# PSUM banks of a second attention: who shares which of four

## The chip, the cores and the metric

The kernel runs on one core of a Trainium2 chip. Its time is the device time in microseconds of one execution; several runs are made, and the median is compared. The core has five engines with queues of their own: PE (TensorE, matmuls, with its weight loads shown as PEld), DVE (VectorE), ACT (ScalarE), POOL (GpSimd) and SP, which issues the DMAs. PE writes its results to PSUM, which has eight banks of 128 x 512 float32; DVE and ACT read them from there. A bank can be given to a new result only when all readers of the old one are done.

## What is computed

The reference is a decoder of two layers on x of 4 x 1024 x 256. Layer 0 is a causal attention with 16 heads of 16 and linear biases, a cross-attention over 77 context rows with 16 heads, and a gated feed-forward with quantised weights. Layer 1 is a power attention with decay, a cross-attention with 8 heads, and a gated feed-forward with blockwise FP4 rounding. The part around the change is the power attention of layer 1:

```python
S = jnp.einsum('bhtd,bhsd->bhts', Q, K)
Tm = DEG * jnp.log(jnp.abs(S) + EPS) + jnp.log(jnp.float32(scale))
Z = Tm + log_G[..., :, None] - log_G[..., None, :]     # log_G: cumulated log of the gates; causal mask
P = jnp.exp(Z - Z_rowmax)
y = jnp.einsum('bhts,bhsd->bhtd', P, V) / jnp.sum(P, axis=-1)[..., None]
```

With DEG = 2 the exponential of Tm is a square, so that P is (|S| + eps) squared times a decay that depends on the two positions.

## The kernel before

The whole computation is one program. Python generators (`A0`, `XA`, `F0`, `A1`, `XF`, ...) emit instructions, and `weave` (L1168) mixes two generators by fixed proportions, so that the attention of one batch row stands beside the cross-attention and the feed-forward of the row before. `schedule` (L1202) has two phases. In phase 0 the attention of layer 0 is the main strand. In phase 1 (`K.phase = 1`) the main strand is `A1`, the power attention, and the side strands are the rest of layer 0 for the last row, the projections of the next row (`A1_front`, which calls `qkv`, L264) and `XF`, the cross-attention and feed-forward of layer 1. After the last attention the feed-forward of the last row runs in four lanes. The order in which the generators emit is only a priority: a scheduler orders each engine's queue when the program is built, by durations that it assumes, and may move any instruction whose operands and buffers allow it. On the chip each engine then works its queue off in that fixed order.

PSUM tiles come from `p(tag)` (L155). It looks up the banks of a tag in `BANKS[self.phase]` (L131 to L134) and takes them in turn; the counter belongs to the tuple of banks, so tags with the same tuple share one turn. Each bank holds one tile at a time. The second dictionary is that of phase 1:

- S: scores of A1 (`scores`, L877). A unit is one key tile of 128 against up to 256 queries for four heads. Its matmuls are at L901, two heads to a tile of 128 x 2 x 256, so a unit has two S tiles. Each is emptied into P (four buffers) with the absolute value: three in four by DVE at L907, one in four by ACT at L905. ACT squares the whole of P at L909, and POOL multiplies diagonal units with the decay at L912. `pv` (L915) multiplies P with V at L930 into O, at least two units later (`LAG1` = 2).
- D: `decay` (L866) makes the decays of a chunk's two diagonal units one chunk ahead: two tiles, each two matmuls at L873 and an exponential by ACT at L874 into y1. `local` (L861) makes the queries' factor for two chunks: a matmul at L863 and an exponential at L864 into `ub`, of which there is one. `a1_gates` (L778) uses D once per row (L791 to L800).
- O: the products, a single bank (7). `out` (L934) empties it with L937, L939 and L940 into `ot`, using `ub`.
- U: the sums in `ot` are transposed at L943 to bring queries back to partitions; DVE takes reciprocals of the norms at L946 and scales at L948 into yy, which POOL adds to X at L950.
- Q: projections of `qkv`: transpositions of the normed input (L235), emptied at L179 and L180, matmuls at L191 inside `mm3`, emptied by ACT at L290, L304 and L306 and DVE at L291. The output projection of the last row of layer 0 uses Q as well (L450).
- T and W: the side strands' tiles, in banks 4 to 6. TB and WB: the same for lanes at the very end, when S, D, U and Q are out of use.

A chunk is 256 queries of four heads: two diagonal units and 2c others for chunk c. There are 64 chunks, 320 units, 640 S tiles.

Of the kernel before, what the change touches and what calls it, by code (L numbers as in the profile page):

```python
# [22 lines left out]
B, T, C = 4, 1024, 256  # L23
NT = T // 128
H = 16
D = 16
# [64 lines left out]
class Kern:  # L91
# [13 lines left out]
    def __init__(self, ctx, tc, ins, out, consts, nb=B):  # L105
# [24 lines left out]

    BANKS = (  # L131
        {"S": (0, 1), "M": (2, 3), "M0": (0, 1, 2, 3), "Q": (2, 3), "U": (0,), "D": (0, 1), "O": (7,), "T": (4, 5, 6), "W": (4, 5, 6)},
        {"S": (0, 1), "Q": (2, 3), "U": (2, 3), "D": (2, 3), "O": (7,), "T": (4, 5, 6), "W": (4, 5, 6), "TB": (0, 1, 2, 3), "WB": (0, 1, 2, 3)},
    )  # L134

    XL = {"xX": "yTh", "R2": "yTl", "M0": "WAh", "M1": "WAl", "U0": "qp", "U1": "qp", "E": "V", "xph": "qr", "xpl": "qr"}
# [1192 lines left out]
```

## Time and profile before

| What | us |
|---|---|
| median of 3 runs | 2400.75 |
| lowest, highest | 2393.45, 2407.63 |
| the profiled execution | 2399.32 |
| its span, first to last instruction | 2397.5 |
| PE busy over the span | 2149.5 (90%) |
| DVE, ACT, POOL busy | 1698.9 (71%), 1637.4 (68%), 1195.4 (50%) |
| first score matmul of A1 (L901) starts | 1262.5 |
| last score matmul of A1 starts | 2245.3 |

An engine is busy when one of its instructions is being executed; PE's instructions overlap, so its busy time is not time at its peak. Idle time of an engine is put down to the instruction that released the waiting one. Weight loads run ahead of their matmuls, so that one stall of PE can show in a row of PEld, in one of PE, or in both. What counts for the change is the stretch between 1262 and about 2250 us, in which the second dictionary of banks is in force for S, D, U and Q.

The costliest groups of that attention are L909 on ACT (320 instructions, 344.6 us), L907 on DVE (480, 285.7 us), L901 on PE (1280, 219.0 us) and L930 on PE in two groups, of which the larger has 3584 instructions and 171.4 us.

### The profile page before, as it was taken

The numbers are of one execution on the slowest core, as the hardware profiler recorded it, in microseconds if no ns is written. First come the engines' busy times: TensorE is split into PE (matmuls) and PEld (weight loads), VectorE is DVE, ScalarE is ACT, GpSimd is POOL, SyncE is SP. The second block draws the span as 40 slices with busy tenths as digits, with TensorE's granted clock in tenths as the row PEclk, the third lists the DMA queues.
The fourth block names the chain that finished last, engine by engine and source line by source line (L and its number), as shares of the span: only waits on it lengthen the run. The fifth ranks groups of instructions, "written<-read, shape, count | busy, mean of one in ns | idle before, by whom it ended". The sixth has DMA issues, their size and how long they took to land.

```text
span 2397.5 us, 51455 instructions
## 1 busy us (share of the span) xinstructions
PE 2149.5 (90%) x19110; PEld 1522.7 (64%) x19110; DVE 1698.9 (71%) x3781; ACT 1637.4 (68%) x4173; POOL 1195.4 (50%) x1942
## 2 busy tenths in 40 slices
PE   6898999998999998999989988899988998898886
PEld 5564557755667754676546765567766776676676
DVE  4776457677766787775756677778767786777776
ACT  4474456676756675665768978887678777888542
POOL 7322212254231442412545457777767787876664
PEclk9898899999999999899989999999999999999897
DMA  8975321223841337312252224412331224442000
GB/s 257 286 193 168 101 72 44 73 64 105 265 105 44 86 95 196 87 44 58 87 174 52 67 70 147 128 39 74 92 104 38 56 88 121 92 98 71 10 10 18
DMA packets 182697, 238.45 MB, mean 99 GB/s; under 512 B 16198, under 2 KB 165846, under 8 KB 175958
## 3 DMA queue, kind: packets, MB, share of 16 engines
q1 hardware_dynamic: 182446, 235.15, 35.5%
q8 instruction: 151, 2.47, 0.4%
q14 instruction: 100, 0.82, 0.1%
HBM read 152.62 MB, written 82.21 MB: 98 GB/s over the span
## 4 chain that ended last, share of the span: by engine, by line
PE 64%; DVE 13%; ACT 8%; DMA 7%; POOL 5%; issue 2%; SPq 1%; DVEq 0%; ACTq 0%; POOLq 0%
PE T L191 11%; PE W L191 9%; PE O L413 7%; PE Q L191 6%; PE O L930 6%; PE S L401 5%; PE M L352 5%; PE S L901 4%; DVE P L907 2%; DVE s_mt L357 2%; PE T L726 2%; PE W L633 1%; ACT P L909 1%; DMA KS<-c_alk 1%; PE M L356 1%
## 5 line engine op out<-in xcount | busy, mean ns | idle before, releaser
L357 DVE TENSOR_REDUCE s_mt<-M 128x1 f32<-128x512 f32 (+3 forms) x608 | 386.1, 655 | 103.9 <-PE M L356 76.2
L404 ACT ACTIVATE P<-S 128x512 f32<-128x512 f32 (+1 forms) x640 | 340.2, 563 | 149.4 <-PE S L401 93.0
L909 ACT ACTIVATE P<-P,eps 128x1024 f32<-128x1024 f32 x320 | 344.6, 1084 | 55.1 <-DVE P L907 52.5
L907 DVE TENSOR_REDUCE P<-S 128x512 f32<-128x512 f32 (+1 forms) x480 | 285.7, 611 | 83.9 <-PE S L901 61.8
L352 PE MATMUL M<-KS,QS 108*128 108x512 bf16 (+3 forms) x768 | 225.6, 339 | 43.3 <-DVE s_mt L357 27.5
L901 PE MATMUL S<-QS,KS 96*128 96x256 bf16 (+1 forms) x1280 | 219.0, 269 | 42.0 <-DVE P L907 35.9
L191 PE MATMUL T<-R,xX 128*128 128x352 f32 (+1 forms) x1136 | 246.8, 332 | 4.9 <-ACT E L622 1.9
L401 PE MATMUL S<-QS,KS 110*128 110x256 bf16 (+1 forms) x1280 | 230.7, 268 | 15.6 <-ACT P L404 8.0
L625 POOL TENSOR_TENSOR E<-E,s_xsm 128x616 f32<-128x616 f32 x64 | 77.8, 1217 | 316.9 <-DVE s_xsm L623 188.3
L413 PE MATMUL O<-P,V 128*32 128x256 f32 (+1 forms) x2560 | 231.4, 374 | 0.1
L191 PEld LDWEIGHTS T<-R,xX 128*128 128x128 f32 x1136 | 183.0, 190 | 25.6 <-ACT E L622 6.5
L912 POOL TENSOR_TENSOR P<-P,y 128x512 f32<-128x512 f32 x128 | 166.5, 1309 | 48.3 <-ACT P L909 28.1
L191 PE MATMUL W<-R,xph 128*128 128x256 f32 (+1 forms) x952 | 184.9, 292 | 3.3 <-ACT xph L179 2.6
L622 ACT ACTIVATE E<-T,s_xmx 128x77 f32<-128x77 f32 x512 | 159.4, 334 | 25.7 <-DVE s_xmx L619 23.0
L930 PE MATMUL O<-P,VsJ 128*32 128x128 f32 x3584 | 171.4, 286 | 5.6 <-ACT P L909 5.3
L901 PEld LDWEIGHTS <-KS 96*128 96x128 bf16 x1280 | 103.9, 99 | 113.4 <-issue 90.6
L401 PEld LDWEIGHTS <-KS 110*128 110x128 bf16 x1280 | 106.4, 100 | 104.9 <-issue 57.2
L191 PEld LDWEIGHTS W<-R,xph 128*128 128x128 f32 (+1 forms) x952 | 149.9, 192 | 12.1 <-issue 3.6
L352 PEld LDWEIGHTS <-QS 108*128 108x128 bf16 x768 | 68.1, 99 | 116.0 <-issue 88.2
L191 PE MATMUL W<-R,xpl 128*128 128x256 f32 (+2 forms) x476 | 139.1, 292 | 1.4 <-DVE xpl L180 1.2
L179 ACT ACTIVATE xph<-W 128x512 fp32r<-128x512 f32 (+2 forms) x180 | 79.6, 459 | 86.6 <-PE W L636 39.6
L733 POOL TENSOR_TENSOR R<-wst 128x256 f32<-128x256 f32 x128 | 92.4, 732 | 83.0 <-DVE wst L732 71.2
(353 smaller groups left out, 5683.8 us busy)
## 6 DMA issues: line engine op xcount, KB each, us to landing
QS<-dr SPq DMA_DIRECT2D x144, 192.0 KB
KS<-dr SPq DMA_DIRECT2D x72, 384.0 KB
dr<-qp SPq DMA_DIRECT2D x32, 768.0 KB
MD<-R SPq DMA_DIRECT2D x24, 616.0 KB
UD<-R SPq DMA_DIRECT2D x24, 512.0 KB
R<-MD SPq DMA_DIRECT2D x32, 308.0 KB
X<-in_x SPq DMA_DIRECT2D x16, 512.0 KB
dr<-qp SPq DMA_DIRECT2D x32, 256.0 KB
```

Of the source, the lines that this page charges most:

```text
L191: nc.tensor.matmul(out, x, y, start=first and n == 0, stop=last and n == len(seq) - 1)
L352: nc.tensor.matmul(Sv[:, x, 0:w], QS[:108, i // 4, hh, i % 4 * 128 : i % 4 * 128 + 128], KS[:108, hh, k0:k1], start=x == 0, stop=not diag ...
L357: nc.vector.tensor_reduce(out, Sv[:, :, 0:w], AX.X, ALU.max)
L401: nc.tensor.matmul(S[:, e, 0:w], st[1][:110, hh, j * 128 : (j + 1) * 128], st[0][:110, q0 // 512, hh, q0 % 512 : q0 % 512 + w], start=e == ...
L404: nc.scalar.activation(P[:, 2 * p : 2 * p + 2, 256 - w :], S[:, :, 0:w], AF.Exp)
L413: nc.tensor.matmul(O[0][hh * 32 : hh * 32 + 32, o + o0 : o + 256], V[j // 4][:, j % 4, h * 17 : h * 17 + 32], P[:, hh, o0:], start=c % 2 = ...
L622: nc.scalar.activation(E[:, n * 77 : (n + 1) * 77], Sv[:, k, :], AF.Exp, bias=mx[:, n : n + 1], accum_out=sm[:, n : n + 1])
L901: nc.tensor.matmul(S[:, e, 0:w], st[r][1][:96, hh, j * 128 : (j + 1) * 128], st[r][0][:96, q0 // 512, hh, q0 % 512 : q0 % 512 + w], start= ...
L907: nc.vector.tensor_reduce(Pv, S[:, :, 0:w].unsqueeze(3), AX.X, ALU.max, apply_absolute_value=True)
L909: nc.scalar.activation(Pw, Pw, AF.Square, bias=self.eps1)
L912: nc.gpsimd.tensor_tensor(Pd, Pd, Ds[r, c][:, j - 2 * c], ALU.mult)
L930: nc.tensor.matmul(Oc[rows, o0 : o0 + 128], lhs, P[:, hh, c0 : c0 + 128], start=j == 2 * c and i == 2 * c, stop=fin and i == 2 * c + 1)
```

## The change

One line of the table of banks, that of phase 1, is replaced.

```diff
     BANKS = (
         {"S": (0, 1), "M": (2, 3), "M0": (0, 1, 2, 3), "Q": (2, 3), "U": (0,), "D": (0, 1), "O": (7,), "T": (4, 5, 6), "W": (4, 5, 6)},
-        {"S": (0, 1), "Q": (2, 3), "U": (2, 3), "D": (2, 3), "O": (7,), "T": (4, 5, 6), "W": (4, 5, 6), "TB": (0, 1, 2, 3), "WB": (0, 1, 2, 3)},
+        {"S": (0, 1, 2), "Q": (2, 3), "U": (3,), "D": (3,), "O": (7,), "T": (4, 5, 6), "W": (4, 5, 6), "TB": (0, 1, 2, 3), "WB": (0, 1, 2, 3)},
     )
```

Before, S turned over banks 0 and 1, and Q, U and D together over 2 and 3. After it, S turns over 0, 1 and 2; U and D turn over bank 3 alone; Q has its own turn over 2 and 3, so every second Q tile lies in a bank of the scores and the others in that of U and D. Nothing else in the source differs. Since the scheduler orders queues by what buffers allow, the order of instructions on every engine differs from the point where phase 1 begins.

## The prediction

> **What bounds the kernel now.** I read the table of stages first, then the waits inside the changed stage, then the costliest groups. The changed table is in force only in the second attention, whose first score matmul starts at 1262 us and whose last evacuation ends near 2248 us, so I cut the span there (columns: stretch, length, then busy us of PE, weight loads, DVE, ACT, POOL, then granted clock, DMA share, GB/s):
> ```profile
> 0.00:1262.00 1262.00, 1143.77 (x8997) 746.99 (x8997) 864.78 (x1910) 785.10 (x2180) 426.61 (x623) 0.96 0.44 124
> 1262.00:2246.00 984.00, 891.29 (x9409) 670.09 (x9405) 732.91 (x1673) 796.42 (x1832) 679.44 (x1216) 0.96 0.31 82
> 2246.00:2397.50 151.50, 114.43 (x708) 105.62 (x708) 101.22 (x200) 55.91 (x162) 89.36 (x104) 0.85 0.03 11
> ```
> In the middle stage PE is busy 891 of 984 us, ACT 796, DVE 733. PE is the bound, closely followed by ACT. PE executes in order, so all that a PSUM bank can give or take here lies in PE's idle 93 us. The waits of that stage say what the idle time waits for (engine, what waited, what it waited for: total us, times, longest us):
> ```profile
> DVE P L907 <- PE S L901: 61.8, 83, 2.2
> PE S L901 <- DVE P L907: 35.9, 55, 3.8
> PEld O L930 <- POOL P L912: 10.0, 23, 1.3
> PEld O L930 <- ACT P L909: 8.3, 24, 1.2
> PE O L930 <- ACT P L909: 5.3, 12, 0.9
> PE S L901 <- ACT P L905: 5.0, 7, 2.5
> PEld L873 <- DVE yy L948: 4.3, 5, 1.8
> PE D L863 <- ACT y L874: 3.6, 3, 2.4
> PE O L930 <- POOL P L912: 3.1, 6, 0.8
> PEld U L943 <- ACT y L874: 1.8, 3, 0.8
> PE D L873 <- DVE yy L948: 1.5, 2, 1.3
> ```
> Two facts stand here. The score matmuls S wait 35.9 + 5.0 = 41 us for L907 or L905 to empty one of their two banks; these are the largest waits of PE. The tiles D, U and Q, which share the other two banks, wait little: rows like L873 behind yy, L863 behind y, U and Q behind y and behind qr or yTl come to about 19 us together (5.8 + 3.6 + 0.9 + 2.8 + 2.1 + 4.0; PE and PEld rows of one stall may overlap, so this is rather too much).
>
> How long one tile holds a bank shows in a stretch of the timeline (start us, us, engine, line, operation):
> ```profile
> 1646.07 0.38 PE L943 MATMUL U<-ident,ot 128*128 128x128 f32 x2
> 1646.77 0.20 DVE L946 RECIPROCAL s_orec<-U 128x8 f32<-128x8 f32 x1
> 1646.95 0.39 PE L873 MATMUL D<-y,DL 96*128 96x256 bf16 x2
> 1647.18 0.28 DVE L948 TENSOR_TENSOR yy<-U,s_orec 128x128 f32<-128x128 f32 x1
> 1649.77 0.61 ACT L874 ACTIVATE y<-D 128x512 f32<-128x512 f32 x1
> 1651.20 0.39 PE L873 MATMUL D<-y,DL 96*128 96x256 bf16 x2
> 1651.63 0.60 ACT L874 ACTIVATE y<-D 128x512 f32<-128x512 f32 x1 [0.22 <-PE D L873]
> ```
> U holds its bank from 1646.07 to 1647.46 (1.4 us). The first D is written at 1646.95, while U is still being read: that needs the second bank. Its exponential starts only at 1649.77, because ACT is in order and stood behind other work, so this D holds a bank for 3.4 us and the next for 1.0.
>
> **The change, part by part.** No instruction of computation is added or removed. S turns over three banks (0, 1, 2), U and D share bank 3 alone, Q still turns over 2 and 3, so every second Q sits among the scores. The scheduler reorders all engines after that. I compared the order of PE's matmuls in the two built programs, which has no times in it, and measured distances in "PE work": the matmuls in between, at the pace that the trace's weight loads and starts show (0.12 us for 128x256 of L191, 0.16 for 128x352, 0.11 for a 256-wide score or decay, 0.03 for one L930). One us of this work takes 984/643 = 1.5 us in the stage. I call a refill tight if under 1.5 us of PE work lies between the last matmul of a bank's old tile and the first of its new one.
>
> S: of 640 tiles, 311 refills are tight before and 234 after (under 1.0 us: 195 and 140). The 41 us scaled by 234/311 lose 10.2, by 140/195 lose 11.6. Bounds: nothing, if the evacuating engines are the limit anyway, and the whole 41. I take -11, because both counts agree.
>
> O: scores now run further ahead of the products that use them. From a unit's last score matmul to its first L930 there is a median of 4.1 us of PE work before and 4.8 after; pairs under 2.0 us fall from 46 to 16, under 2.5 from 77 to 41. PE's waits at L930 are 8.4 us by the PE rows and 20 by the weight loads' rows (POOL, ACT and the small ones). 8.4 x 0.47 = 4 to 20 x 0.65 = 13; I take -8, the middle. Bounds: 0 and -20.
>
> D, U, Q: tight refills rise from 71 to 118, under 1.0 us from 42 to 74. Largest is D after D (20 to 44: the two halves of one decay tile, formerly in two banks). 19 us scaled by 118/71 add 13, by 74/42 add 15: I take +14. What waits behind a stopped D on PE is everything, the scores included. L863 (the decay of the queries, exponent in `ub`, needed by L937 before the single O bank is free) formerly waited for ACT in 27 of its 32 places; now it waits for DVE in 31, that is, for the U of the chunk before. Bounds: below, 0, since the scheduler has put other matmuls between; above, every one of 118 waits as long as the rows now last (5.8 us in 7 waits, 0.83 each): 98, so +79.
>
> Beside the path: the DMA issues that SP has to make for the gates (L855, L859) and the stacks move by a few places against each other; the queue's share is 0.31 in this stage, and I cost them at nothing; if DL or DR came late, L873 would wait as in its 6.2 us (3.6 + 2.6) now, and I allow the same once more in the range. At the end, 96 us of PE work stand behind the last score instead of 88. The tail runs 151.5/88 = 1.7 us per us of work against 1.5 in the stage: 8 x 0.2 gives +1.5.
>
> Sum: -11 - 8 + 14 + 1.5 = -3.5. The profiled execution took 2399.3 us (span 2397.5 and 1.8 around it), so 2396 us; that is 5 us under the median of the runs, 2400.75.
>
> A rule to weigh: the Trainium skill, "Perfetto Trace Analysis", section "Matmuls", says that independent matmul groups should rotate through several banks, so that the evacuation of one lies beside the matmuls of the next. The row of S behind L907 agrees with it; but the change breaks the same rule for D and U. By the rule alone, one would count groups: 640 S tiles gain a bank, 160 D and 64 U tiles lose one, and the change would be a plain gain up to the 41 us. The rows of the waits, with order, say that the two sides about cancel.
>
> **Rivals.**
>
> *The single bank takes over (slower).* D, U and L863 form one chain through bank 3: products end, ot, U's transposition, L946 and L948, then L863 or L873, its exponential, then the next D. About 64 chunks in 984 us make 15.4 us for each; U 1.4 + D 3.4 + 1.0 + half of L863 fill some 6.5 of it, and while projections run every second Q, with twelve matmuls and two readers of 0.6 and 0.7 us, lies in it too. For it: ACT is 81% busy and in order, so a D can be held for over 3 us, which the order alone does not tell. Against it: decays are made one chunk ahead. Now 71 tight refills give about 24 waits, a third. If half of 118 wait 0.83 us, that is 49 - 19 = +30, and with -19 + 1.5 the time is 2412; with two thirds (65 us) 2428. It decides from half upwards; price 2420.
>
> *Three banks free the scores (faster).* DVE idles 61.8 us for S. If S's waits fall by three quarters (-31), O's by 13 and D's rise by 14, with 1.5 for the tail, the time is 2371. For it: PE is the bound and S the largest wait. Against it: 234 refills remain tight.
>
> *The wait only changes its name (no change).* P has four buffers. The first score of a unit now starts before the buffer it will be evacuated to is out of use (under 0.5 us of PE work after the L930 of four units before) in 207 of 316 units, against 75. A full third bank then waits for P rather than S for a bank: S and O gains vanish by half, -9 + 14 + 1.5, 2406.
>
> **How the numbers follow.** Forecast 2396, own range 2386 to 2408: chance 0.38, of which 0.08 falls over 0.5% faster. No change by P: 0.04. Faster rival: 0.24. Slower rival: 0.34. A difference under 0.5% (12 us) is about what a measurement of this kernel can't tell from none. So faster 0.32, same 0.34, slower 0.34. For 8 times in 10 the range reaches down to 2366 (a little beyond the faster rival) and up to 2430 (two thirds of the tight refills waiting, 2428, and a little for DMA).
>
> **What would show it.** In the waits of the stage: PE S behind L907 at 26 us rather than 36, behind 10 it is the faster rival; L873, L863, U and Q behind yy, y and qr at 33 us, over 55 it is the slower one; the waits of L930 halved. A new row of DVE P L907 or ACT P L905 behind PE O L930 (11.6 and 5.2 now) at over 30 would be the wait for P. I would be wrong altogether if the time moved outside the stage, before 1262 us, or in the tail by more than a few us.

## The result and the profile after

The changed kernel takes 2415.2 us (median of 13 runs, 2406.2 to 2422.7) against 2400.4 for the kernel before (13 runs beside them): 1.0067 times, with a 95% interval of 1.0053 to 1.008. The forecast was 2396, a little faster.

The table of stages of the changed kernel, cut where its own score matmuls begin and end (columns as in the prediction):

```profile
0.00:1267.60 1267.60, 1145.28 (x8973) 748.91 (x8999) 863.90 (x1911) 786.15 (x2182) 426.66 (x623) 0.95 0.43 123
1267.60:2262.90 995.30, 881.56 (x9328) 670.53 (x9337) 714.71 (x1660) 788.02 (x1823) 674.51 (x1211) 0.96 0.31 81
2262.90:2414.90 152.00, 115.59 (x778) 106.48 (x777) 106.37 (x212) 60.22 (x170) 88.95 (x108) 0.91 0.04 15
```

and the kernel before, cut at its own first and last score matmul:

```profile
1262.50:2245.30 982.80, 890.79 (x9404) 669.92 (x9404) 731.71 (x1671) 795.29 (x1830) 679.36 (x1215) 0.96 0.31 82
2245.30:2397.50 152.20, 114.75 (x710) 105.66 (x710) 101.92 (x201) 56.55 (x163) 89.36 (x104) 0.85 0.03 11
```

The two spans differ by 17.4 us. About 5 lie before the second attention, where both programs have the same order on every engine, so they are chance of these two executions. The stage of the attention is 12 us longer, the tail as long as before although PE has 68 instructions more in it.

The waits of the stage in the changed kernel, the rows that answer those of the prediction, and four that the prediction had not read:

```profile
ACT y L874 <- PE D L873: 23.1, 24, 2.6
POOL P L912 <- ACT y L874: 25.9, 21, 3.8
PE S L901 <- DVE P L907: 25.4, 52, 1.7
PEld O L930 <- POOL P L912: 19.6, 35, 2.7
DVE P L907 <- PE O L930: 19.2, 25, 2.6
ACT P L905 <- PE O L930: 14.8, 12, 2.5
PE O L930 <- POOL P L912: 9.6, 12, 2.2
PE D L873 <- ACT y L874: 6.9, 9, 1.7
PEld U L943 <- ACT y L874: 6.4, 7, 1.5
PE D L863 <- DVE yy L948: 2.9, 2, 1.8
PE S L901 <- ACT P L905: 2.8, 7, 0.7
```

The same four of the kernel before:

```profile
POOL P L912 <- ACT y L874: 19.9, 9, 10.6
DVE P L907 <- PE O L930: 11.6, 10, 3.3
ACT y L874 <- PE D L873: 9.1, 16, 1.9
ACT P L905 <- PE O L930: 5.2, 6, 1.8
```

Three things are to be seen. The wait of S for its evacuation by L907 and L905 fell from 41 to 28 us, as the bank should make it. ACT now idles 23 us at L874 for a decay's matmul, 9 before, and PE waits 6.9 us at L873 for L874, 0.9 before: ACT stands at bank 3 for longer than PE. And DVE and ACT idle 34 us, 17 before, until L930 gives a buffer of P free. A stretch of the changed kernel shows the first of these standstills (the last bracket is the idle time ahead of the instruction and what ended it):

```profile
1752.15 0.60 ACT L874 ACTIVATE y<-D 128x512 f32<-128x512 f32 x1
1752.80 0.38 PE L873 MATMUL D<-y,DL 96*128 96x256 bf16 x2
1752.82 1.65 POOL L912 TENSOR_TENSOR P<-P,y 128x512 f32<-128x512 f32 x1 [0.28 <-ACT y L874]
1753.21 0.60 ACT L874 ACTIVATE y<-D 128x512 f32<-128x512 f32 x1 [0.47 <-PE D L873]
```

The second half's matmuls cannot start before the first half's exponential has left the bank (1752.75); ACT has nothing it may do in between, since its order is fixed, and waits 0.47 us.

If all of PE's own rows in the stage are added up by the tile that waits, PE idles 20.6 us more than before: S -7.4 (the rows above give -13; waits for the readers of Q, which now shares bank 2, take back about 5), D, U, Q and L863 +11.3, O +4.3, and T and W, whose banks were not touched, +12.4 (17.1 to 29.5). The busy time of PE in the stage fell by 9, which leaves some 12.

### The profile page after: what moved, and what is told of

It reads as the page before. It is cut to its first block, busy times and chain, and to the rows that moved or that the text cites. A ratio compares the mean times of both kernels' runs of the same rounds, so it can differ in the third digit from the quotient of the medians.

```text
span 2414.9 us, 51582 instructions
## 1 busy us (share of the span) xinstructions
PE 2142.4 (89%) x19076; PEld 1525.9 (63%) x19110; DVE 1685.0 (70%) x3781; ACT 1634.4 (68%) x4173; POOL 1190.1 (49%) x1942
## 4 chain that ended last, share of the span: by engine, by line
PE 61%; DVE 14%; POOL 8%; DMA 7%; ACT 6%; issue 2%; SPq 1%; POOLq 0%; DVEq 0%; ACTq 0%
PE T L191 10%; PE W L191 8%; PE O L413 7%; PE O L930 5%; PE Q L191 5%; PE S L401 5%; PE M L352 5%; PE S L901 3%; DVE P L907 2%; DVE s_mt L357 2%; POOL P L912 2%; PE W L633 1%; PE T L726 1%; PE M L356 1%; PE S L403 1%
## 5 line engine op out<-in xcount | busy, mean ns | idle before, releaser
L909 ACT ACTIVATE P<-P,eps 128x1024 f32<-128x1024 f32 (+1 forms) x320 | 342.5, 1094 | 33.1 <-DVE P L907 30.9
L907 DVE TENSOR_REDUCE P<-S 128x512 f32<-128x512 f32 (+1 forms) x480 | 283.3, 610 | 88.8 <-PE S L901 61.3
L901 PE MATMUL S<-QS,KS 96*128 96x256 bf16 (+1 forms) x1280 | 207.8, 267 | 35.6 <-DVE P L907 25.4
L912 POOL TENSOR_TENSOR P<-P,y 128x512 f32<-128x512 f32 x128 | 167.4, 1314 | 49.0 <-ACT y L874 25.9
L930 PE MATMUL O<-P,VsJ 128*32 128x128 f32 x3584 | 167.4, 283 | 1.8 <-ACT P L909 1.7
```

The source lines that it names most:

```text
L901: nc.tensor.matmul(S[:, e, 0:w], st[r][1][:96, hh, j * 128 : (j + 1) * 128], st[r][0][:96, q0 // 512, hh, q0 % 512 : q0 % 512 + w], start= ...
L907: nc.vector.tensor_reduce(Pv, S[:, :, 0:w].unsqueeze(3), AX.X, ALU.max, apply_absolute_value=True)
L909: nc.scalar.activation(Pw, Pw, AF.Square, bias=self.eps1)
L912: nc.gpsimd.tensor_tensor(Pd, Pd, Ds[r, c][:, j - 2 * c], ALU.mult)
L930: nc.tensor.matmul(Oc[rows, o0 : o0 + 128], lhs, P[:, hh, c0 : c0 + 128], start=j == 2 * c and i == 2 * c, stop=fin and i == 2 * c + 1)
```

## The experiments

In all of them the one line of the table of banks is edited, unless a diff says more. Times are medians; each ratio is to runs of the kernel before on the same chip.

**The two halves of the change.** Theory A: the single bank of U and D costs the time. Theory B: the third bank of S costs, by letting scores run ahead. Theory C: only the new order of the queues.

```diff
-{"S": (0, 1), "Q": (2, 3), "U": (2, 3), "D": (2, 3), ...
+{"S": (0, 1, 2), "Q": (2, 3), "U": (2, 3), "D": (2, 3), ...   # e1_scores_three
+{"S": (0, 1), "Q": (2, 3), "U": (3,), "D": (3,), ...           # e2_single_bank
```

> S turns over banks 0, 1, 2; D, U and Q stay together on 2 and 3, as before the change. Theory A (the single bank for D and U costs the time): D and U keep two banks, so most of the loss goes: 2396 to 2404 us, L873, U and Q wait about as before plus what S in bank 2 takes from them. Theory B (scores that run ahead on a third bank push the side strand's evacuations on DVE and ACT back): the loss stays, 2410 to 2420, and the waits of PE at T and W stand near 30 us of the stage as after the change, against 17 before. Theory C (only another order): anything between 2390 and 2420, with no tie to S or D.

> S keeps two banks; U and D share bank 3, Q turns over 2 and 3. Theory A: the loss shows without the third bank, and is larger since the gain of S is missing: 2415 to 2425, D, U and Q waits of PE up by 11 us, S near 41. Theory B: no loss, 2396 to 2406, waits at T and W near 17 us. Theory C: anything between 2390 and 2420.

e1: 2448.8 us, 1.0213 (1.019 to 1.0235). e2: 2447.9 us, 1.0205 (1.0181 to 1.0228). In these orders each half alone costs three times what both cost together; no theory had said so. The rows of e1 show a loss of its own at the products (10.0, 8.3, 3.1 and 5.3 us in the kernel before):

```profile
PEld O L930 <- POOL P L912: 22.8, 32, 2.0
PEld O L930 <- ACT P L909: 17.7, 36, 1.3
PE O L930 <- POOL P L912: 12.3, 19, 1.7
PE O L930 <- ACT P L909: 9.6, 18, 1.3
```

S in bank 2 shares it with D, U and Q, so one of a unit's two score tiles waits where the other does not. In e1's order a median of 3.7 us of PE work lies between the first and the last score matmul of a unit, 0.8 in the kernel before, and P is late for L930. Its tail has 224 instructions into T and W left, 338 in the kernel before, so this third bank did not let the scores pass the side strand. So e1 prices a bad neighbour rather than a third bank; one order of it was run. e2's rows are in part those of theory A:

```profile
ACT y L874 <- PE D L873: 34.1, 34, 4.0
PE S L901 <- DVE P L907: 29.0, 53, 2.3
```

The rows of D, U, Q and L863 on PE rose to 36 us, 23 before, as A said. The wait of S for L907 and L905 did not stay near 41 but is 34, with two banks. And of the 68 us by which e2's attention stage is longer (1051 and 983), PE's idle rows hold only 22. The rest is in PE's busy time, 936 us against 891: 112 instructions more, and 98 ns for each on the mean instead of 95. What made them longer was not found.

**The order by itself.** The same sharing with numbers exchanged or turns begun at another bank.

```diff
+{"S": (2, 3), "Q": (0, 1), "U": (0, 1), "D": (0, 1), ...      # c1_banks_swapped, as before
+{"S": (1, 0), "Q": (3, 2), "U": (3, 2), "D": (3, 2), ...      # c2_turn_flipped, as before
+{"S": (2, 3, 0), "Q": (0, 1), "U": (1,), "D": (1,), ...       # c3_after_permuted, as changed
+{"S": (1, 2, 0), "Q": (3, 2), "U": (3,), "D": (3,), ...       # c4_after_flipped, as changed
+{"S": (1, 0), "Q": (3, 2), "U": (3,), "D": (3,), ...          # e2b_single_flipped, as e2
```

> The map of before with numbers exchanged: S on 2 and 3, Q, U and D on 0 and 1. Every tag has as many banks and the same partners as before; only the places at the phase's ends and so the order that the scheduler finds differ. Theories A and B: 2396 to 2405, no difference. Theory C: a difference of the size of the change's own, 10 us or more to either side.

> The map of before with each turn begun at the other bank: S on 1, 0; Q, U and D on 3, 2. A second reordering of the old sharing. If orders of one sharing scatter little (as the first exchange, 2398), 2393 to 2405; if they scatter as the two orders of the changed sharing did (2415 and 2437), 2380 to 2425.

> The map of the changed kernel with numbers exchanged: S on 2, 3, 0, Q on 0 and 1, U and D on 1. The same sharing, another order. Theories A and B: 2410 to 2420, as the changed kernel. Theory C: a time apart from the changed kernel's by 10 us or more, possibly at or below that of before.

> The map of the changed kernel with turns begun elsewhere: S on 1, 2, 0, Q on 3, 2, U and D on 3. A third order of the new sharing. If the sharing is what costs, over 2405, between or near 2415 and 2437. If the change's loss is an accident of its order, as likely under 2400 as over.

> The sharing of e2 (S on two banks, U and D on 3) with the turns begun at the other bank: a second order. If 2448 was the sharing, 2430 to 2460; if it was mostly its order, 2405 to 2425.

The stage is that from the first to the last score matmul, the tail what follows it, both in the profiled execution. The last column counts PE's instructions into tiles T and W that are left for the tail.

| sharing | times of its orders, us | mean | stage | tail | T, W in the tail |
|---|---|---|---|---|---|
| as before | 2400 (before), 2398 (c1), 2414 (c2) | 2404 | 983, 974, 1011 | 152, 150, 139 | 338, 338, 248 |
| as changed | 2415 (after), 2437 (c3), 2434 (c4) | 2429 | 995, 1011, 1012 | 152, 159, 156 | 392, 416, 378 |
| as e2 | 2448 (e2), 2430 (e2b) | 2439 | 1051, 1029 | 134, 140 | 224, 248 |

Orders of one sharing lie up to 22 us apart, so theory C holds for the size: the 15 us between the two kernels is itself a draw. Their sharings differ by about 25 on the mean of three orders each. They overlap at the edge: c2, the slowest of the old, is 1.007 times the kernel before (1.0056 to 1.0084), and the changed kernel, the fastest of the new, 1.0067. The signs in the waits hold in all six: ACT behind L873 8 to 11 us in the old sharing and 23 to 33 in the new; DVE and ACT behind L930 9 to 17 and 34 to 40; PE's idle rows of the stage 86 to 92 in sum and 109 to 110. c1 is as the kernel before: 0.9998 (0.9985 to 1.0011). Not all of a longer stage is idle time of PE: c2's is 28 us longer than the stage of the kernel before, with 3 us more in PE's idle rows and 26 more of busy time (917 and 891, with 90 instructions more and a granted clock of 0.95 against 0.96).

**Who may be D's neighbour.**

```diff
+{"S": (0, 1), "Q": (2, 3), "U": (2,), "D": (3,), ...           # e6_d_alone
+{"S": (0, 1, 2), "Q": (2, 3), "U": (4, 5, 6), "D": (3,), ...   # e10_u_to_side
```

> S keeps 0 and 1; D alone on bank 3, U alone on bank 2, Q turns over 2 and 3. Against e2 (U and D together on 3, 2448 us) only U is moved out. Theory A1 (D waits for the chain through U's readers on DVE): most of the loss goes, 2400 to 2415, and ACT's wait at L874 for the matmuls of D falls from 34 us to near 9. Theory A2 (the two halves of a decay tile follow each other in one bank, and ACT in its fixed order stands behind the second): the loss stays, 2430 to 2450, with ACT's wait at L874 at 25 us or more.

> The changed kernel with U moved from bank 3 to the turn of T and W (4, 5, 6): D is alone on 3 but for every second Q. Theory A1 (U and D in one bank make the loss): at or under the kernel before, 2385 to 2402 us. Theory A2 (D after D makes it): little gained, 2408 to 2418.

Theory A1 says that U and D in one bank make the loss, A2 that the two halves of a decay in one bank do. e6: 2411.3 us, 1.0045 (1.0029 to 1.0061): 19 to 37 us under the two orders of e2, by moving U out of D's bank. ACT's row behind D is below e2's 34.1 us, but no lower than that of e2b, 23.0:

```profile
ACT y L874 <- PE D L873: 22.7, 26, 3.6
PE S L901 <- DVE P L907: 26.6, 55, 2.8
```

So both A1 and A2 were half right: the time went down as A1 said, while a standstill at L874, which A2 named, stayed far above the 9 us of the kernel before. It seems to cost little by itself, as e6 stands only 7 us above the old sharing's mean; but e6 is a single order, and 7 us is within the scatter of orders. e10 is the slowest map with T and W at three banks: 2513.9 us, 1.0469 (1.0443 to 1.0495). U in the turn of T and W holds up the side strand (PE's rows at T and W come to 85 us, 17 before). It tells nothing on U and D.

**A third bank that no other tile uses**, taken from T and W, read against a kernel in which it is taken and left unused.

```diff
+{"S": (0, 1, 6), ... "T": (4, 5), "W": (4, 5), ...   # e7_third_from_side
+{"S": (0, 1), ... "T": (4, 5), "W": (4, 5), ...      # e8_side_two
```

> S on 0, 1 and 6, a third bank that nothing else uses; T and W keep only 4 and 5; D, U and Q on 2 and 3 as before the change. To be read against e8, which takes the same bank from T and W and gives it to nobody. Theory A (an undisturbed third bank helps S; the loss is all in D and U): 20 to 35 us under e8, as the changed kernel is 33 under e2. Theory B (scores that run ahead harm by themselves): no better than e8, or worse.

> T and W on 4 and 5 alone, bank 6 unused in the second attention, all else as before. It only prices the bank that e7 takes: 2410 to 2480 us by either theory, since T and W hold over half of PE's matmuls there.

e8: 2560.2 us, 1.067 (1.0644 to 1.0695); e7: 2572.5, 1.0715 (1.069 to 1.0739). The undisturbed third bank made the kernel 12 us slower, where theory A wanted 20 to 35 faster. The stages of e8, then of e7:

```profile
1262.50:2345.70 1083.20, 904.70 (x9242) 672.45 (x9241) 710.25 (x1628) 790.50 (x1806) 661.23 (x1202) 0.93 0.28 73
2345.70:2557.40 211.70, 143.69 (x872) 130.20 (x871) 121.33 (x244) 68.50 (x187) 101.10 (x118) 0.82 0.05 17
```
```profile
1255.00:2321.50 1066.50, 883.34 (x9193) 664.64 (x9195) 689.86 (x1598) 775.20 (x1744) 653.80 (x1207) 0.93 0.28 73
2321.50:2571.00 249.50, 169.64 (x1023) 152.53 (x1022) 137.76 (x282) 84.31 (x265) 112.61 (x126) 0.83 0.06 19
```

The scores begin 7.5 us sooner and end 17 us sooner after they began, and the tail is 38 us longer, with 151 more instructions of PE in it. By tile, 636 instructions into T and W are left for the tail, 501 in e8: the scores have moved forward past the side strand, whose rest is then done when little else stands beside it (PE busy 68% of the tail, 83% of the stage).

**The steps read apart, without U.** The transposition of the sums and its readers are left out, so the output lacks the norms and is in the wrong place. Bank 3 of the last two kernels then holds the decays, L863's tile and every second Q.

```diff
-ps = self.p("U")[:, :256] ... nc.vector.reciprocal(r, pv_[:, :, :, 16])
-nc.vector.tensor_tensor(y, pv_[:, :, :, 0:16], r..., ALU.mult)
+nc.vector.tensor_copy(y, ot[:, 0:128].rearrange("p (q h e) -> p q h e", q=2, h=4))
 # n_before_no_u: banks as before; n_mid_no_u: S (0, 1), D (3,), Q (2, 3); n_after_no_u: banks as changed
```

> The kernel before, with the transposition of the sums, the reciprocal and the scaling left out: L943, L946 and L948 are replaced by one copy of a part of ot into yy on DVE. It prices U in the old sharing: its 126 transpositions take about 13 us of PE work, at 1.5 us of time each some 15 to 20 us less than before, 2380 to 2388, by both theories.

> The changed kernel with the same part left out, so that D is alone on bank 3 but for every second Q. Theory A1 (U and D in one bank make the loss, and the third bank gains): at or under the other kernel without U, 2360 to 2385. Theory A2 (two halves of a decay in one bank, ACT standing behind the second, make it): the gap of 15 us to the other kernel without U stays, 2393 to 2405.

> Without U as the two kernels before it; S on 0 and 1, D on 3 alone, Q on 2 and 3. It stands between the kernels without U of old (2393) and new sharing (2424). Theory A2 (D in a single bank costs): near 2420 or above, and the third bank of S then adds little. Theory B (the third bank of S costs, through the wait for P): near 2395 to 2403, and the step to 2424 is the third bank's. One order scatters by some 10 us to either side.

2392.9 us (0.998, 0.9964 to 0.9996; 2380 to 2388 was expected), then 2411.0 (1.0049, 1.0033 to 1.0065) with D in one bank, then 2424.1 (1.0108, 1.009 to 1.0125) with the third bank of S. A1 falls as the whole cause: without U the gap is 31 us, not less. Both steps cost, 18 and 13. The stages of the first, the second and the third kernel show where:

```profile
1262.30:2253.70 991.40, 890.98 (x9327) 667.85 (x9326) 748.34 (x1621) 797.05 (x1838) 689.17 (x1219) 0.95 0.31 81
2253.70:2391.40 137.70, 99.98 (x660) 93.29 (x659) 89.10 (x186) 52.36 (x155) 84.38 (x101) 0.88 0.04 12
```
```profile
1261.90:2270.60 1008.70, 906.20 (x9333) 677.62 (x9332) 749.24 (x1624) 801.56 (x1837) 688.90 (x1220) 0.94 0.30 80
2270.60:2409.20 138.60, 99.38 (x652) 91.93 (x652) 90.11 (x184) 53.22 (x156) 81.52 (x99) 0.90 0.04 12
```
```profile
1260.60:2261.90 1001.30, 872.61 (x9187) 663.40 (x9186) 726.17 (x1593) 783.98 (x1818) 675.57 (x1210) 0.93 0.31 80
2261.90:2420.60 158.70, 121.54 (x798) 113.13 (x798) 109.76 (x215) 62.82 (x175) 93.05 (x109) 0.89 0.04 14
```

D's single bank makes the stage 17 us longer and leaves the tail as it was; 15 of the 17 are busy time of PE (906 and 891, with the granted clock at 0.94 and 0.95), and PE's idle rows are 99 and 97. The third bank gives 7 of the stage back and adds 20 to the tail, with 146 more PE instructions there (414 into T and W, 284 without it), as in e7. One order each, so either step is known to some 10 us.

**Without D, and a fifth buffer of P.** All decays but the first are left out; POOL multiplies with the first one's. Then two of three places for the decays' right-hand side are free, and every fifth P can lie there.

```diff
 def decay(r, b, g, c):
+    if Ds:
+        Ds[r, c] = next(iter(Ds.values()))
+        return
     # n_before_no_d, n_after_no_d; with what follows n_before_five_p, n_after_five_p
-    P = self.t([128, 4, 256], F32, "P")
+    self.np = getattr(self, "np", -1) + 1
+    P = self.t([128, 4, 256], F32, "y0" if self.np % 5 == 4 else "P")
     ...
-    t = self.t([128, 2, 512], F32, "y0")
-    for k in range(2):
-        add_dr(t[:, k])
```

> The kernel before with the decays of all chunks but the first left out (L873, L874; POOL multiplies with the first one's). ACT has 75 us less to do, PE some 25 of work. It gives the base for the next: 2350 to 2390 by both theories.

> The changed kernel with the same decays left out; bank 3 then holds U, L863's tile and every second Q. Theory A2 (D in one bank costs): at or under the kernel without decays of old sharing, -10 to +5 us. Theory B (the third bank costs): the gap stays, 15 to 35 us above it, with DVE and ACT behind L930 for 30 us or more together.

> The kernel before without decays, with every fifth P in the buffer y0, which held two of the three copies of the right-hand side of the decays: five buffers of P instead of four. Theory B (the wait for P): little, 2360 to 2375, since the waits of DVE and ACT behind L930 are only 10 us with two banks of S. If P were the limit of the old sharing too, under 2355.

> The changed kernel without decays, with the same fifth P. Theory B (the third bank costs because DVE and ACT then wait for a buffer of P): the gap of 20 us closes, at most 8 us above the other kernel with five P, and the waits of DVE and ACT behind L930 fall from 28 to under 15 us. If the wait for P is only a sign and the third bank costs by letting the scores pass the side strand, the gap stays at 12 us or more.

Without D: 2370.2 us (0.9872, 0.9855 to 0.9889) and 2390.5 (0.9962, 0.995 to 0.9974). The gap of 20 us stays when no decay is left for bank 3 to stop, against A2 as the whole cause (U, L863's tile and Q still share it). The scores take nearly as long in both (958 and 962 us); the tail is 147 and 165, with 338 and 420 instructions into T and W:

```profile
2220.80:2368.00 147.20, 111.43 (x709) 102.74 (x707) 97.70 (x199) 56.97 (x163) 87.36 (x103) 0.87 0.03 12
```
```profile
2222.60:2387.60 165.00, 126.30 (x807) 117.66 (x806) 111.40 (x228) 64.22 (x178) 94.13 (x111) 0.85 0.04 14
```

With the fifth P: 2377.7 us (0.9913, 0.9898 to 0.9928) and 2427.2 (1.0104, 1.0081 to 1.0128). The first is 8 us slower than with four, where little change was expected. The gap did not close, it grew to 50, although DVE and ACT waited less for P in the changed sharing: 20.3 us (below; L905, L907 and L930 are L909, L911 and L934 in this kernel) against 27.6 with four.

```profile
ACT P L909 <- PE O L934: 11.3, 9, 4.6
DVE P L911 <- PE O L934: 9.0, 9, 2.2
```

So the wait for P is not the way in which the changed sharing costs: it became shorter and the gap wider. The tail went up once more, to 173 us in the profiled execution, with 444 instructions into T and W. That execution was one of the shorter ones of its kernel (2413 us; four of six lie at 2427 to 2430), so its rows do not account for the whole of the growth, and where the rest sits stays open.

## Why the prediction was wrong

- *The bound.* PE as the bound of the stage, and S behind L907 as its largest wait: right. The step that failed is the conclusion: that all a bank can give or take lies in PE's idle time, counted only at the tiles whose banks or products were touched. T and W had no term in the sum and went from 17 to 29.5 us in the pair of profiles; O was put at -8 and came to +4.3. Each of the two is some 12 us off. Forecast (-3.5) and pair (+12 from the first score on) lie 16 apart; S, 4 us short, adds to the two, and D, U and Q, the tail and PE's busy time take the rest back. Nor does all of a loss lie in idle time: the stages of c2, e2 and n_mid grew by 28, 68 and 17 us, PE's idle rows by 3, 22 and 2.
- *How it reaches T and W* is inferred, not shown. Instructions of ACT and DVE stand in a fixed order too, and they are 81% and 74% busy, so what they lose at one tile can show up on PE at another. In the prediction's own stretch, ACT stood idle for 1.67 us at L1097 (1648.93), waiting for a matmul into T, before it came to D at 1649.77. T and W wait 17 to 26 us in the old sharing's three orders and 29 to 34 in the new one's. But the standstill at L874 alone does not set this: e2b has 23 us of it and 21 at T and W, c2 11 and 26.
- *S, -11.* Mechanism right, size nearly: -7 over all that S waits for. Behind L907 and L905 alone S waits 38 to 41 us in the old sharing's orders and 26 to 33 in the new one's; but with two banks e6 has 31 and e2b 47, so no single pair shows the bank alone. And this wait was not worth its length, since part of it or more returns in the tail, where the side strand that was passed is left: in the kernels without U, -7 in the stage and +20 after it; in e7 against e8, -17 and +38; on the means of the orders of e2's sharing and the new one, -34 and +18.
- *O, -8.* Wrong sign: +4 on PE, and PEld behind POOL from 10 to 20. The order did put more PE work between scores and products, but by the rows DVE and ACT were late by waiting for P, and POOL by waiting for L874 (25.9 us in 21 waits, 19.9 in 9 before).
- *D, U, Q, +14.* +11 by PE's rows, so nearly right there; unpriced was ACT's standstill at L874, +14 in this pair and +12 to +25 in the others. The single bank's whole cost is about 35 us (means of e2's two orders and of the old sharing's three), 18 without U and 7 with U in another bank (one order each).
- *The tail, +1.5.* In this pair 0, on the mean of three orders each +9 (147 and 156 us). It was priced as a change of pace for 8 us of work; the stage did not shrink by what was moved out of it: PE's busy time there fell by 9 us and its idle rows rose by 21.
- *The rivals.* "The single bank takes over" named the right loss, and its 2412 lies near the measured time, but by luck: the rows of D, U, Q and L863 reached 35 us on PE, not the 55 that it set. "The wait only changes its name" was right in its row: DVE and ACT behind L930 for 34 us, over the 30 that it set; it was given 0.04. Its mechanism, P as the limit, did not hold: with a fifth P the wait became shorter and the gap wider. "Three banks free the scores" failed against the kernel before. Beside the single bank of U and D the third bank does gain: 33 us from e2 to the changed kernel, none from e2b to c4, 10 on the means.
- *The rule that was weighed* (the Trainium skill, "Perfetto Trace Analysis", section "Matmuls": independent groups of matmuls should rotate through several banks). The counts of groups would have made a gain of up to 41 us. Its mechanism shows, S waits 13 us less behind L907 and L905; its gain does not, in this kernel nor in e7, where the scores got a bank of their own and the kernel became 12 us slower.
- *Not considered:* that a new order by itself moves the time by up to 22 us. A forecast of 3.5 us from counts in one order could not have been better than its sign.

What the runs show: the new sharing costs, about 25 us on the mean of three orders, of which the kernel here shows 15; every pair of old and new sharing that was run, with U and D or without one of them, has the new one slower, but for c2, which equals the changed kernel. U and D in one bank make the attention stage longer: 1029 and 1051 us in the two orders of e2's sharing, 974 to 1011 in the old. The third bank of S does not make up for it. With U it takes some 34 us off the stage and adds 18 to the tail on the means, and without U it takes 7 off and adds 20. So the price of a step is not additive, and it is not settled beyond some 10 us. That the side strand is passed is read from the instructions into T and W that are left for the tail (338, 338 and 248 in the old sharing; 392, 416 and 378 in the new); no experiment holds the side strand's place while S has three banks, so what this costs by itself stays open. No map tried beats the kernel before.

## What to carry to other kernels

Where a scheduler fixes the order of strands that share engines, a buffer given to one strand can also be priority: before you count the waits it removes, ask which strand will be passed, and what stands beside the rest of that strand at the end. Be wary of putting a tile of slow readers into the turn of a fast one (e1, e10). Read the waits of the engine that empties a bank as well as PE's, and PE's busy time as well as its idle time. And measure two or three neutral reorderings before you believe a difference under one per cent: here renumbered banks alone made 2398 or 2414.

## What the runs showed of the hardware beyond that

The granted clock of the stage lay at 0.92 (e10) to 0.97 (n_before_no_d), at 0.96 in both kernels of the pair, so it has no visible part in their difference. It may have some in others: among 212 runs, each compared with the other runs of its kernel, a run took 1.1 us more for each 0.001 of mean granted clock that it had less. The mean clock was 0.950 in n_before_no_u and 0.941 in n_after_no_u, and 0.951 and 0.939 in the two kernels with five P. If the same slope holds between kernels, which was not tested, an estimate from these numbers puts about 10 of the 31 us and 13 of the 50 us down to the clock; for the old and the new sharing (0.950 and 0.948 on the mean of orders) it is 3 of 25. Whether a lower clock makes the longer time, or more idle time the lower clock, is open.

The mean of L907 was 611 ns before and 610 after. One size was a surprise: the third bank of T and W is worth 160 us (e8, expected at 10 to 80), over three times the largest difference that a map of the attention's four banks made (50 us, e1).
